# A two-layer graph attention kernel: 128-row transposes and block-diagonal products cut into 64-row tiles, two links of the step loop moved one step later, and the gathers of a group released at two places

## The chip, the cores and the metric

One core of a Trainium2 chip runs the kernel. The time is device microseconds of one execution, as the median of repeated runs. The engines of the core are named as in the profile: PE is TensorE (matrix products and transposes), PEld the loading of its stationary operands, DVE is VectorE, ACT is ScalarE, POOL is GpSimd (it also issues the gathers), and SP is SyncE, which here only issues DMAs.

## The reference

Two graph attention layers over 2048 nodes with the same 0/1 adjacency matrix, for a batch of 8 inputs with 64 features each. The first layer has 4 heads, the second one.

```python
def _gat_layer(h, mask, b):
    scores = jnp.einsum('...nd,...md->...nm', h, h)
    scores = jnp.where(mask, scores, NEG)
    attn = jax.nn.softmax(scores, axis=-1)
    return jnp.einsum('...nm,...md->...nd', attn, h) + b

mask = graph + jnp.eye(N, dtype=graph.dtype) > 0
h = jnp.einsum('bnc,hdc->bhnd', x, Wh)              # 8 x 4 x 2048 x 64
out_h = _gat_layer(h, mask[None, None], bh[None, :, None, :])
z = jax.nn.leaky_relu(cat, negative_slope=0.2)      # cat: the 4 heads side by side
h2 = jnp.einsum('bnk,dk->bnd', z, Wo)               # 256 features back to 64
out2 = _gat_layer(h2, mask[None], bo)
z2 = jax.nn.leaky_relu(out2, negative_slope=0.2)
...                                                 # layer norm, times gamma, plus beta
x = _layernorm(x + out)
```

## The kernel before

The adjacency is sparse but for its first nodes. The kernel treats 56 nodes as hubs, with dense products. The other 1992 nodes are cut into 166 sets of 12. For each set the kernel finds a list of at most 128 nodes that any of the 12 is linked to (the picks: chains of MAX8 and MATCH_REPLACE8 on DVE, L727 to L784), and only those are gathered. A step of the first layer works on one group of two sets, so there are NG = 83 groups; a step of the second layer works on four sets, 42 steps.

In the trace the hub stage lasts from 0 to about 162 us, the first layer's stage (called stage 1 here) from 162 to about 634, a passage between the layers to about 680, and the second layer's stage (stage 2) to about 1017, followed by the end of the layer norms.

A gathered set is a tile `g` of 128 nodes by 4 pairs of batches, with 128 features for each pair (two batches side by side), 64 KB and more. What stage 1 does with group g, in the order of the data:

- **gather** (L790): two indirect DMAs, one for each set, issued by POOL into buffers of a pool of 10, which is 5 groups.
- **turn** (L509): per set four transposes of 128x128, node rows to feature rows, into the PSUM tile with tag T. ACT copies it to `xTg` (L1030).
- **own_rows** (L795, a POOL copy per two groups), **columns** (L802, PE) and **keep_columns** (L808, ACT): the 12 nodes' own rows times the Gram matrix of each head. The stationary operand is block-diagonal: both batches of a pair in one 128x128 product, half of it zeros.
- **scores** (L814, PE, tag S): 32 products on 64x64 tiles, four of them standing abreast in the matrix engine. **weigh** (L824, DVE) subtracts the mask, **lift** (L831, ACT) takes the exponential.
- **values** (L837, PE, tag O): 16 products on 128x64 tiles, two abreast; each pair's first or last column gives the softmax sums. **invert** (L848, DVE) divides.
- **turn_values** (L859, PE): four transposes of 112x128 into a free corner of the same tile of tag O; **keep_values** (L865, ACT, two copies) brings them out.
- **project** (L525, PE, tag C) and **leaky** (L514, ACT), **leak** (DVE): the 4 heads' weights on 64x64 tiles; **second_maps** (L873, PE) and **keep_own** (L882): the second layer's input; **second_rows** (L889, PE, one transpose of 128 rows) and **keep_rows** (L892, DVE): back to node rows, which SP writes to the table that stage 2 gathers from.

The order of the work is written out by hand: a loop `for i in range(-4, NG + 3)` (L1017) interleaves different groups, and each engine runs its instructions in the order in which the loop issues them. In the kernel before, step i issues for PE: scores of group i+1, project of i-1, values of i, second_maps of i-2, second_rows of i-3, columns of i+4, turn of the first set of i+3, turn_values of i, turn of the second set of i+3. The gathers of group i+5 are both issued after values of i, and the buffers they write are those of group i, so they wait for the last product of values(i). PSUM is full: four tags S, C, O and T, each one buffer of two banks. Also in the loop are the list jobs of the later rounds (`some(n)` does n of them; one job is a MAX8 with its MATCH_REPLACE8), parts of the hubs' work in the first eight steps (`slow`), and from step 30 on the loading of x and the adding of beta for the end (`load_own` on SP, `add_beta` on POOL).

In the hub stage `turn_x` (L580) transposes x itself with the same `turn`. In stage 2 `turn2` (L1314) turns two groups a step with the same `turn`, 16 transposes, an ACT copy of 128x1024 behind each eight (L1320); `scores2` (L1126) reads the copies.

Of the kernel before, what the change touches and what calls it, by code (L numbers as in the profile page):

```python
# [44 lines left out]
HUB = 56  # L45
# [314 lines left out]
def fast_kernel(ctx: ExitStack, tc: tile.TileContext, x, adj, Wh, bh, Wo, bo, gamma, beta, out, flag):  # L360
# [148 lines left out]
    def turn(tp, rows):  # L509

        for q in range(Q):
            nc.tensor.transpose(tp[:, q * P:(q + 1) * P], rows[:, q, 1:1 + P], ident)  # L512
# [12 lines left out]
    def project(ot, cat, n):  # L525

        for hp in range(HP):
            for s in range(2):
                for j in range(2):
                    h = 2 * hp + j  # L530
                    nc.tensor.matmul(cat[half(j), s, hp * n:(hp + 1) * n], whT[half(s), h * D:(h + 1) * D],  # L531
                                     ot[half(s), h, :], start=True, stop=True)
# [47 lines left out]
    def turn_x(i):  # L580
        tp = two(f"px{i}")
        turn(tp[:, 0, :], xrow[i])
        nc.scalar.copy(xT[:, :, i * P:(i + 1) * P], tp[:, 0, :].rearrange("c (q n) -> c q n", q=Q))
# [143 lines left out]
    def pick(r):  # L727
# [7 lines left out]
        def top(src, dst, last):  # L735
            def job():
                nc.vector.max(out=dst, in_=src)
                if not last:
                    nc.vector.match_replace(out=src, in_to_replace=dst, in_values=src, imm_value=-1.0)
            return job  # L740

        for j in range(ns):
            for i in range(KEEP // 8):
                k = j * KEEP + i * 8
                todo.append(top(kv[:, j, :], cand[:, k:k + 8], i == KEEP // 8 - 1))
# [7 lines left out]
        for i in range(P // 8):  # L753
            todo.append(top(cand, best[:, i * 8:(i + 1) * 8], i == P // 8 - 1))
# [35 lines left out]
    def gather(table, s, layer, new):  # L790
        t = rows[layer, s] = new(f"g{layer}_{s}")
        nc.gpsimd.indirect_dma_start(out=t.rearrange("n q c -> n (q c)"), out_offset=None, in_=table,  # L792
                                     in_offset=bass.IndirectOffsetOnAxis(ap=index[:, s:s + 1], axis=0))

    def own_rows(m):  # L795

        w = min(4, NS - 4 * m)
        t = held["x", m] = work.tile([P, 2 * GM], F32, tag="xo", name=f"xo{m}", bufs=2)
        src = xT[:, :, HUB:].rearrange("c q (k s) -> c s q k", s=NS)[:, 4 * m:4 * m + w]
        nc.gpsimd.tensor_copy(t[:, :w * 48].rearrange("c (s q k) -> c s q k", s=w, q=Q), src)  # L800

    def columns(g, cat):  # L802

        n = min(4, NS - 4 * (g // 2)) * 48
        for k in range(2):
            nc.tensor.matmul(cat[:, k, 2 * GM:2 * GM + n], gram[:, g % 2 * 2 + k, :], held["x", g // 2][:, :n], start=True, stop=True)  # L806

    def keep_columns(g, cat):  # L808
        n = min(4, NS - 4 * (g // 2)) * 48
# [624 lines left out]
```

## Time and profile before

| what | value |
|---|---|
| median of 14 runs | 1046.41 us (1036.43 to 1052.23) |
| the profiled execution, own time | 1054.11 us |
| its span on the core | 1052.2 us |
| its mean granted PE clock | 0.916 |
| stage 1, 349 to 560 us: PE busy | 207.09 of 211.00 us |
| stage 1, 349 to 560 us: DVE, ACT, POOL busy | 130.84, 135.76, 120.79 us |
| stage 2, 700 to 1000 us: PE busy | 229.55 of 300.00 us |
| stage 2, 700 to 1000 us: DVE, ACT, POOL busy | 163.36, 146.71, 132.04 us |

The profile page lists the busy time of each engine, the chain of work that ended last, and groups of instructions: one row for each line and operation, with the count behind "x", then after a bar the busy time in us and the mean of one in ns, and after a second bar the idle time of that engine just before them and what ended most of it. The timeline lists an engine's blocks in order of time: start in us, duration in us, engine, line, operation, moving and stationary operand, tile of the matrix engine (rows*columns), the instruction's shape, count. Matrix instructions are pipelined, so blocks overlap by the depth of the pipe, and the time of a block is best read from its start to the next block's start. An fp32 product counts as two instructions, a transpose as one.

### The profile page before, as it was taken

Reading aid. Unit: us, or ns where it says so; the run is one execution under the profiler, and the core shown is the slowest. Engines: PE = TensorE matmul, PEld = TensorE weight load, DVE = VectorE, ACT = ScalarE, POOL = GpSimd, SP = SyncE. Lnnn points to the kernel's source line nnn. Section 1 sums busy time; section 2 is a strip of 40 time slices with the busy share of each in tenths; the row PEclk is TensorE's granted clock in tenths of the full one; section 3 lists DMA queues with packets and bytes.
Section 4 is the critical chain, followed back from the end, with each engine's and each line's share of the span. In section 5 each row is a group of like instructions: output and inputs, shape, how many; then the busy total and the mean of one; then the engine's idle time right before and its main releaser. Section 6 shows DMA issues by size and latency. Waiting matters only on the chain.

```text
span 1052.2 us, 42066 instructions
## 1 busy us (share of the span) xinstructions
PE 840.7 (80%) x18437; PEld 709.6 (67%) x18437; DVE 612.8 (58%) x1369; ACT 518.0 (49%) x961; POOL 464.1 (44%) x612
## 2 busy tenths in 40 slices
PE   2977778798999999999999983677787787877740
PEld 2645557687899888888898963466566666666630
DVE  3348844688877777655555553024454555556695
ACT  2322235465666666666666651345444544445541
POOL 5543214564444555555565505344444344444400
PEclk9988889999999999999999995689889899899985
DMA  8775412553344555555555406464555555555521
GB/s 177 226 208 164 123 48 77 150 143 103 98 114 115 146 149 145 153 156 156 153 150 156 126 24 176 131 163 133 153 155 159 152 160 158 143 166 157 162 59 32
DMA packets 81794, 145.22 MB, mean 138 GB/s; under 512 B 30146, under 2 KB 46466, under 8 KB 81602
## 3 DMA queue, kind: packets, MB, share of 16 engines
q0 software_dynamic: 26720, 88.55, 31.4%
q1 hardware_dynamic: 37842, 49.65, 16.3%
q10 hardware_dynamic: 17040, 4.25, 2.2%
q8 instruction: 147, 2.41, 0.9%
q14 instruction: 45, 0.37, 0.1%
HBM read 123.91 MB, written 18.48 MB: 135 GB/s over the span
## 4 chain that ended last, share of the span: by engine, by line
PE 66%; DVE 11%; issue 6%; ACT 6%; DMA 4%; another core or an unknown queue 3%; POOL 1%; SPq 0%; DVEq 0%; ACTq 0%; POOLq 0%
PE t L512 14%; PE s L821 10%; PE o L846 8%; PE cat L806 5%; PE s L1133 5%; PE cat L531 3%; PE o L863 3%; PE o L1165 3%; PE cat L880 3%; ACT xTg L1320 2%; PE sh L1277 2%; PE e L1144 2%; PE cat L890 2%; DVE e L594 1%
## 5 line engine op out<-in xcount | busy, mean ns | idle before, releaser
L792 POOL DMA_INDIRECT g<-table,index x332 | 330.4, 995 | 408.5 <-PE o L846 169.2
L512 PE MATMUL t<-ident,g 128*128 128x128 f32 x1328 | 199.7, 282 | 23.8 <-DMA g<-table,index 12.5
L512 PEld LDWEIGHTS t<-ident,g 128*128 128x128 f32 x1328 | 159.2, 145 | 42.6 <-issue 34.7
L1320 ACT COPY xTg<-t 128x1024 f32<-128x1024 f32 x83 | 80.7, 1016 | 132.3 <-PE t L512 85.4
L826 DVE TENSOR_TENSOR e<-s,mask 128x768 f32<-128x768 f32 x83 | 79.5, 957 | 105.7 <-PE s L821 105.3
L821 PE MATMUL s<-y,xTg 64*64 64x48 f32 x5312 | 115.1, 222 | 4.6 <-issue 3.4
L821 PEld LDWEIGHTS s<-y,xTg 64*64 64x64 f32 x5312 | 98.9, 134 | 24.4 <-issue 15.5
L1152 DVE TENSOR_TENSOR es<-e,linked 128x384 f32<-128x384 f32 (+1 forms) x42 | 23.1, 551 | 144.8 <-PE t L512 93.7
L518 ACT ACTIVATE z<-cat,bhp 128x192 f32<-128x192 f32 x166 | 60.9, 418 | 85.7 <-PE cat L531 85.7
L846 PE MATMUL o<-g,e 128*64 128x65 f32 x2656 | 96.5, 226 | 0.0
L1133 PE MATMUL s<-xTg,bd 128*32 128x128 f32 x1328 | 66.3, 318 | 32.6 <-issue 20.1
L846 PEld LDWEIGHTS o<-g,e 128*64 128x64 f32 x2656 | 84.9, 139 | 9.9 <-issue 0.2
L1030 ACT COPY xTg<-t 128x1024 f32<-128x1024 f32 x83 | 84.1, 1013 | 2.4 <-PE t L512 2.4
L833 ACT ACTIVATE e<-e,shifts 128x768 f32<-128x768 f32 x83 | 79.3, 955 | 2.1 <-DVE e L826 2.0
L1133 PEld LDWEIGHTS s<-xTg,bd 128*32 128x32 f32 x1328 | 43.8, 126 | 50.0 <-issue 40.4
L597 ACT ACTIVATE e<-e,shifts 128x896 f32<-128x896 f32 x32 | 33.4, 1044 | 83.2 <-DVE e L594 68.2
L812 ACT COPY y<-cat 128x384 f32<-128x384 f32 (+1 forms) x80 | 40.7, 508 | 65.9 <-DVE rowt L894 41.5
L680 POOL TENSOR_SCALAR a<-raw 120x1024 bf16<-120x1024 int32 (+1 forms) x34 | 37.9, 1119 | 67.0 <-DMA raw<-in_adj_dram 36.5
L806 PE MATMUL cat<-xo,gram 128*128 128x192 f32 (+1 forms) x320 | 65.0, 326 | 0.0
L1165 PE MATMUL o<-g,es 128*32 128x65 f32 x2656 | 57.7, 244 | 8.1 <-DVE y_s L1188 5.1
L1165 PEld LDWEIGHTS o<-g,es 128*32 128x32 f32 x2656 | 53.0, 126 | 10.5 <-issue 6.2
L853 DVE RECIPROCAL rall<-o 64x8 f32<-64x8 f32 x166 | 34.0, 205 | 44.1 <-PE o L846 42.7
(177 smaller groups left out, 1462.8 us busy)
## 6 DMA issues: line engine op xcount, KB each, us to landing
raw<-in_adj_dram SPq DMA_DIRECT2D x32, 480.0 KB
table<-xb SPq DMA_DIRECT2D x22, 256.0 KB
xr_s<-table SPq DMA_DIRECT2D x21, 256.0 KB
g<-table,index POOLq DMA_INDIRECT x332
table<-x SPq DMA_DIRECT2D x16, 260.0 KB
x<-in_x_dram ACTq DMA_DIRECT2D x32, 128.0 KB
table<-rowt SPq DMA_DIRECT2D x166, 24.4 KB
xb<-in_x_dram SPq DMA_DIRECT2D x164, 24.0 KB
```

Of the source, the lines that this page charges most:

```text
L512: nc.tensor.transpose(tp[:, q * P:(q + 1) * P], rows[:, q, 1:1 + P], ident)
L518: nc.scalar.activation(z[:, hp], cat[:, :, hp * n:(hp + 1) * n], AF.Identity, bias=bhp[:, hp:hp + 1], scale=1.0)
L792: nc.gpsimd.indirect_dma_start(out=t.rearrange("n q c -> n (q c)"), out_offset=None, in_=table, in_offset=bass.IndirectOffsetOnAxis(ap=ind ...
L806: nc.tensor.matmul(cat[:, k, 2 * GM:2 * GM + n], gram[:, g % 2 * 2 + k, :], held["x", g // 2][:, :n], start=True, stop=True)
L821: nc.tensor.matmul(sp[half(r), p, (q * 2 + j) * M:(q * 2 + j + 1) * M], xt[half(p), j, q, half(r)], y[half(p), (j * Q + q) * M:(j * Q + q ...
L826: nc.vector.tensor_tensor(e[:, :16 * M].rearrange("p (a q n) -> p a q n", a=2, q=Q), sp[:, :, :8 * M].rearrange("p a (q n) -> p a q n", q= ...
L833: nc.scalar.activation(e[:, :16 * M], e[:, :16 * M], AF.Exp, bias=shifts[:, 0:1], scale=1.0)
L846: nc.tensor.matmul(op[half(p), j, o0:o0 + K1], e[:, c0:c0 + 64], rw[j][:, q, sums(p)], start=True, stop=True)
L1030: nc.scalar.copy(t, held.pop(("tp", i + 2)))
L1133: nc.tensor.matmul(sp[q * 32:(q + 1) * 32, k, :], bd[u % 3][:, k, q, :], xt[:, s % 2, q, :], start=True, stop=True, tile_position=(0, q * 32))
L1165: nc.tensor.matmul(op[t * 32:(t + 1) * 32, f, k * W2 + p:k * W2 + p + K1], e[:, 2 * q + p, k, :], rw[:, q, sums(p)], start=(a == 0 and k = ...
L1320: nc.scalar.copy(t, tp)
```

## The change

- `turn` makes two transposes of 64 node rows out of each of 128: stationary 64x128, moving a 64x64 identity. The two halves write to two banks of the tile. This holds for stage 1, for the hub stage and for stage 2; the readers take a view (`turned_rows`) in which the halves lie apart.
- `columns` becomes eight products on 64x64 tiles with 96 columns each in place of two block-diagonal products of 128x128 with 192. It writes to the tile of tag O, not C, and stands ahead of values. `own_rows` makes three POOL copies in place of one: half of the rows are also needed with the two batches swapped.
- `turn_values` becomes eight transposes of 48x128 in place of four of 112x128, done one step later (group i-1 in step i) and written to the tile of tag C; `keep_values` is one ACT copy in place of two. Project, leaky and leak (group i-2), second_maps (i-3, into the tile of tag S) and second_rows (i-4, two transposes of 64 rows) follow a step later. The loop runs to NG + 4, one step more.
- The first gather of group i+4 is issued at the start of step i and waits for turn_values of the step before; the second is issued after values(i) and waits for project of step i. Both waits are added by hand.
- A list job is one MAX8 or one MATCH_REPLACE8, not a pair. Six jobs run in each step with i < 0 (none before), three in a step up to 15, then two. `load_own` and `add_beta` start at step 10 and run in four steps of six, not at step 30 in each step in turn.
- PE's order in step i is now: scores i+1, project i-2, columns i+4, values i, second_maps i-3, turn_values i-1, second_rows i-4, turn of both sets of i+3.

On all engines together PE gets 2311 more matrix instructions (664 for the turns of stage 1, 664 for those of stage 2, 64 for `turn_x`, 504 for columns, 332 for turn_values, 83 for second_rows), ACT 83 fewer, POOL 84 more; DVE and SP keep their number.

The diff, cut to what is spoken of:

```diff
-    def turn(tp, rows):
+    def turn(tp, rows, j=0):
         for q in range(Q):
-            nc.tensor.transpose(tp[:, q * P:(q + 1) * P], rows[:, q, 1:1 + P], ident)
+            c0 = (j * Q + q) * 64
+            for r in range(2):
+                nc.tensor.transpose(tp[:, r, c0:c0 + 64], rows[half(r), q, 1:1 + P], ident[half(r), half(r)])
...
-    def gather(table, s, layer, new):
+    def gather(table, s, layer, new, behind=None):
...
+        if behind is not None:
+            tc.add_manual_dep(g.ins, behind.ins.name, mybir.DependencyInfo(mybir.DependencyClass.Sync, mybir.DependencyReason.DATA),
+                              reason="the gather's turn")
...
-        nc.gpsimd.tensor_copy(t[:, :w * 48].rearrange("c (s q k) -> c s q k", s=w, q=Q), src)
+        nc.gpsimd.tensor_copy(v[:, 0], src[:, 4 * m:4 * m + 2])
+        b0 = min(4 * m + 2, NS - 2)
+        for r in range(2):
+            nc.gpsimd.tensor_copy(v[half(r), 1], src[half(1 - r), b0:b0 + 2])
...
-            nc.tensor.matmul(cat[:, k, 2 * GM:2 * GM + n], gram[:, g % 2 * 2 + k, :], held["x", g // 2][:, :n], start=True, stop=True)
+            for r in range(2):
+                for p in range(2):
+                    nc.tensor.matmul(op[half(p), r, Q * OW + k * GM:Q * OW + (k + 1) * GM], gram[half(r), g % 2 * 2 + k, half(r)],
+                                     t[half(r), (p ^ r) * GM:((p ^ r) + 1) * GM], start=True, stop=True)
...
-    def turn_values(g, op):
+    def turn_values(g, pt):
-        osb = held.pop(("o", g))
+        osb = held.pop(("o", g)).rearrange("a j q c -> a (j q c)")
         for w in range(4):
-            nc.tensor.transpose(turned(op)[:, w, :], osb[:112, w].rearrange("a s c -> a (s c)"), ident[:112, :112])
+            for p in range(2):
+                mine = slice(p * 64, p * 64 + M)
+                at = nc.tensor.transpose(pt[:, p, w * M:(w + 1) * M], osb[mine, w * P:(w + 1) * P], ident[mine, mine])
+        return at
...
     def second_rows(g, pr):
-        nc.tensor.transpose(pr, held.pop(("own", g)), ident)
+        t = held.pop(("own", g))
+        for r in range(2):
+            nc.tensor.transpose(pr[:, r, :], t[half(r)], ident[half(r), half(r)])
...
-    LOOK = 5
+    LOOK = 4
...
-    for i in range(-4, NG + 3):
+    for i in range(-4, NG + 4):
+        coming = i + LOOK if i > 0 else i + LOOK + 1 if -2 <= i < 0 else NG
+        if coming < NG:
+            gather(table1, 2 * coming, 1, rows_tile, turned_at)
...
-            project(held.pop(("ot", i - 1)), cat, GM)
+            projected_at = project(held.pop(("ot", i - 2)), cat, GM)
...
+            columns(i + 4, op)
         if 0 <= i < NG:
-            op = one(f"o{i}", "O")
             values(i, op)
-            invert(i, op)
-        if 0 <= i + LOOK < NG and i > -3:
-            for j in range(2):
-                gather(table1, 2 * (i + LOOK) + j, 1, rows_tile)
+        if coming < NG:
+            gather(table1, 2 * coming + 1, 1, rows_tile, projected_at)
...
-        if 0 <= (i - 30) // 2 <= NV:
-            (add_beta if i % 2 else load_own)((i - 30) // 2)
+        if i >= 10 and (i - 10) // 6 * 2 + (i - 10) % 6 // 2 <= NV and (i - 10) % 6 < 4:
+            (add_beta if i % 2 else load_own)((i - 10) // 6 * 2 + (i - 10) % 6 // 2)
+        quota = 6 if i < 0 else 3 if i < 16 else 2
...
+            turned_at = turn_values(i - 1, cat[:, :, 2 * GM:4 * GM])
...
-            turn(tp[:, 0, :], rows[1, 2 * (i + 3)])
-        if 0 <= i < NG:
-            turn_values(i, op)
-            keep_values(i, op)
-        if 0 <= i + 3 < NG:
-            turn(tp[:, 1, :], rows[1, 2 * (i + 3) + 1])
+            for j in range(2):
+                turn(tp, rows[1, 2 * (i + 3) + j], j)
```

## The prediction, made before the changed kernel had run

> **What bounds the kernel now.** I read the table of stretches first, because the busy shares of the whole span mix stages with different limits. Its columns are: stretch, PE busy and its count, PEld, DVE, ACT and POOL in the same way, PE's granted clock, DMA share, GB/s.
>
> ```profile
> 264.00:349.00 85.00, 84.36 (x2201) 76.62 (x2199) 66.19 (x181) 54.65 (x113) 40.12 (x54) 1.00 0.43 110
> 349.00:560.00 211.00, 207.09 (x5334) 185.94 (x5332) 130.84 (x330) 135.76 (x273) 120.79 (x156) 1.00 0.55 153
> 700.00:1000.00 300.00, 229.55 (x4393) 187.85 (x4392) 163.36 (x293) 146.71 (x258) 132.04 (x134) 0.90 0.57 155
> ```
>
> In stage 1 PE is busy for 84.36 of 85 and 207.09 of 211 us at full clock, and no other engine is above 78%. In stage 2 PE is busy for 77%, so there it waits as well. Next comes the chain that ended last, cut to 264 to 349 us: scores L821 23.9%, values L846 19.1%, turns L512 16.7%, columns L806 12.3%, turned values L863 7.7%, and 0.1% issue. It is PE from end to end. Between 700 and 1000 us the turns L512 are 23.0% of the chain (69 us) and the ACT copies behind them, L1320, 8.1%.
>
> Third, PE's timeline of one step of stage 1 (start, duration, and so on to the count):
>
> ```profile
> 312.50 1.37 PE L821 MATMUL s<-y,xTg 64*64 64x48 f32 x63
> ...
> 313.69 0.56 PE L531 MATMUL cat<-otb,whT 64*64 64x96 f32 x15
> 314.19 1.15 PE L846 MATMUL o<-g,e 128*64 128x65 f32 x32
> 315.17 0.50 PE L880 MATMUL cat<-z,woT 128*64 128x96 f32 x8
> 315.60 0.31 PE L890 MATMUL cat<-ident,own 128*96 128x128 f32 x1
> 315.75 0.82 PE L806 MATMUL cat<-xo,gram 128*128 128x192 f32 x4
> 316.40 0.60 PE L512 MATMUL t<-ident,g 128*128 128x128 f32 x4
> 316.84 0.55 PE L863 MATMUL o<-ident,osb 112*128 112x112 f32 x4
> 317.23 0.60 PE L512 MATMUL t<-ident,g 128*128 128x128 f32 x4
> 317.76 0.33 PE L821 MATMUL s<-y,xTg 64*64 64x48 f32 x8
> ```
>
> From each start to the next: scores 1.19, project 0.50, values 0.98, maps 0.43, rows 0.15, columns 0.65, turn 0.44, turned values 0.39, turn 0.53 us. The sum is 5.26 us, and no block waits. So a step lasts as long as PE's own work, and what PE is spared in stage 1 comes off the end until another engine is late.
>
> **The change part by part.** *Rates, from single starts in the same step.* A transpose with 128 moving columns follows the one before it after 109 ns, one with 112 after 95 to 100. Columns (192 moving, one tile) take 163 ns an instruction. All are 0.85 ns a moving column. On 64x64 tiles four instructions stand abreast: project (96 moving) spends 82 ns on four, thus 0.85 ns a column for four tiles together. Scores spend about 58 ns on four with 48 moving columns, and values 58 ns on two with 65. A change of tiling costs about 0.1 us (turn to scores 0.20 for 0.11).
>
> *Columns.* Before, 4 instructions took 0.65 us. After, 16 instructions of 96 columns on 64x64 tiles are project's own shape and stand right behind project with no change of tiling: 4 x 82 ns = 0.33. Project loses the change behind it (0.50 to about 0.36), and columns pay it ahead of values (0.42). Both together go from 1.15 to 0.78: **-0.37 us** a step.
>
> *Turns.* Eight transposes of 109 ns and a change of tiling are 0.97 us. After, 16 halves in two row tiles. The trace has no row tile that is 128 columns wide, so its price is bounded. If halves overlap, as scores' tiles do, a pair lasts for its 64 moving columns, 55 ns: 0.44 + 0.1 = 0.55. If the load of 128 columns paces the pair, L863 is the nearest row: its instructions load 128 columns and follow each other after 95 ns, so the load lasts at most 95 ns, 8 x 95 + 100 = 0.86. If halves don't overlap, 16 x 109 = 1.74 + 0.1 = 1.84. I take 0.55, as L821 shows tiles in both row halves loading and running at once: **-0.42**, with ends -0.42 and +0.87.
>
> *Turned values and rows.* Eight transposes of 48 columns in four pairs: at 58 ns (scores' pace for 48 columns) 0.25 for 0.39, **-0.14**; the ends are 0 (pairs at 95) and 8 x 95 = 0.76, +0.37. Rows are one pair for 0.15: **-0.09**, ends -0.09 and +0.07.
>
> A rule speaks against these two terms. The Trainium skill, page "TensorE: Matmul & The Clock Gate", section "LDWEIGHTS (loading the stationary operand)", says that loading goes by the columns, columns / 1.2 ns, and that 32 rows take as long as 128. By it a half costs 107 ns of loading like the whole, pairs gain nothing if the load paces them, and the sum would end near 1020. The row of L863 (95 ns with 128 columns loaded) lies under that figure, so at least for transposes it doesn't hold in full.
>
> The trace has a row for that side too: early on, at half the pace, L575's products (128 loaded, 112 moving) follow each other every 213 ns, no quicker than transposes with 128 moving at that point, which is a pace by loaded columns. It is a product, L863 a transpose, so I side with L863.
>
> *The sum of a step:* 5.26 - 0.37 - 0.42 - 0.14 - 0.09 = **4.24 us**, -1.02.
>
> *The others in 4.24 us.* ACT: copy 1.01, leaky 2 x 0.42, lift 0.96, columns 0.51, turned values 0.54 = 3.8, less some 0.1 for the copy that goes. DVE: 0.96 + 0.42 + 0.69 + 0.55 + 0.25 + 0.28 = 3.15, and two list jobs (0.41 and 0.50) make 4.06, which just fits; three, up to step 15, make 4.5. POOL: two gathers of 1.0 with 0.3 around each, L886 0.28, own_rows 0.36 + 2 x 0.28 in every second step, 3.3 in all; `add_beta` adds 1.28 in two steps of six, 3.8 on average. SP only issues: two table writes 1.24 and four loads of 0.37 at times, under 3. The hidden work thus has 0.2 to 0.5 us to spare, and where that is gone each 0.1 us costs 8 us over 83 steps.
>
> *The added waits.* The first gather's releaser, turn_values, lies in the step before and has run when POOL arrives. The second waits for project, some 1.6 us into the step; behind it stand own_rows, L886 and `add_beta`. A group must have landed when it is turned, about 1.8 steps (7.6 us) after the first gather and 1.3 (5.5) after the second; gathers land 2.3 to 3.4 us after they start. I cost the waits at 0; with that cover gone, up to 0.5 us a step. DMA goes from 153 to some 190 GB/s, and the hub stage moved 202 in its first 60 us.
>
> *Later steps of the chain.* PE meets turned values, project, maps and rows a step later, so no late ACT or DVE result holds it; nothing is gained, since nothing stalls there now. One more drain step: +2 us.
>
> *Over the stage.* Steps 16 to 82: 67 x 1.02 = 68, of which I keep 64, as some are longer already (5.3 to 5.7 with `load_own` and `add_beta` in them). Steps 0 to 15 carry hub work and three list jobs (DVE 4.5, PE 5.9 in the first nine): I keep about half of 16 x 1.02, 9. Together -73.
>
> *Stage 2.* Each step turns 16 blocks: 16 x 109 = 1.74 us, in the trace 2.2 to 4.2 with stalls that end by issue. Halves save 16 x 54 = 0.87 less the change of tiling, 0.76 x 42 = 32 us if all is on the path. The ACT copies of 1.01 behind the turns don't shrink, and the issue stalls may go by instruction, of which there are now more; I take two thirds, **-21** (ends +49, as below, and -32). In the hub stage `turn_x` is hidden by hub work: 0.
>
> **Sum:** 1054.1 (the profiled execution's own time; span 1052.2) - 73 - 21 + 2 = 962. That execution lies 7.7 above the median of the runs, so 962 - 7.7 = **954** for the median.
>
> **The rivals.** (1) *The load paces the pairs.* For: L575, and L512's and L863's moving columns nearly as many as the loaded. Against: L863. Columns keep -0.37; at 95 ns a pair the turns keep -0.11, else 0. Some 75 full steps: 1054 - 75 x 0.37 to 0.48 + 2, stage 2 0 to -6: 1014 to 1028, so 1006 to 1020 after 7.7. (2) *Another engine or PE's instruction supply becomes the bound.* For: DVE at 4.06 and POOL above 4.24 in some steps; PE issues some 338 instructions and loads a step for 274, in 4.24 us in place of 5.26, and the stalls by issue in stage 2 show that supply can be late. Against: scores alone run 128 in 1.19 us without a hole. At 4.75 us a step: 83 x 0.5 = 41, stage 2 10 to 0: about 1000. (3) *The halves don't overlap,* the slower side: each pays its own 109 or 95 ns. Step: -0.37 + 0.87 + 0.37 + 0.07 = +0.94, x 83 = +78; stage 2 +1.74 x 42 x 2/3 = +49; 1181, so 1173. In stage 1 it decides from about 145 ns a pair (13 pairs x (145 - 115) make up for 0.37). Against it: L821's four tiles share 58 ns.
>
> **How the numbers follow.** Forecast 0.56 (its own range 925 to 985), rival 1 0.15, rival 2 0.20, rival 3 0.09. The low end has all of 83 x 1.02 and 32 on the path: 1054 - 85 - 32 + 2 - 8 = 931, with 11 of spread: 920. The high end takes in rivals 1 and 2 with some spread, 1030. Only rival 3 and little else is outside. A difference of 0.3% is about what a measurement of this kernel can tell from none. Faster than that 0.87 (nearly all of the first three), within it 0.03 (rivals 1 and 2 gone further), slower 0.10.
>
> **What would show it.** In the profile after: in a step of stage 1 turns from start to next start near 0.55, turned values 0.25, project with columns 0.78, steps of 4.2 to 4.3 us, PE still busy above 95%. Right for rival 1: pairs every 95 to 107 ns; for rival 2: PE busy below 92% and DVE, POOL or issue named ahead of PE's blocks; for rival 3: single halves 95 to 109 ns apart. The forecast falls if a step is above 4.5 us, or if turns in stage 2 still take 2 us.

## The result and the profile after

The changed kernel takes 1138.65 us (median of 10 runs, 1128.55 to 1144.11) against 1046.76 for the kernel before: 8.75% longer, ratio 1.0875 with a 95% interval of 1.0846 to 1.0903. The forecast was 954. Its profiled execution takes 1132.33 us, 78 more than that of before. (The latter lies 7.7 us above its kernel's median, so the difference of the medians is 92.)

The page of the changed kernel (engines; then the chain that ended last, by engine and by line):

```profile
PE 829.2 (73%) x21252; PEld 681.3 (60%) x21252; DVE 616.9 (55%) x1369; ACT 566.2 (50%) x878; POOL 482.0 (43%) x696
...
PE 48%; issue 13%; DVE 13%; ACT 8%; DMA 6%; another core or an unknown queue 6%; POOL 3%; SPq 1%; POOLq 0%; DVEq 0%; ACTq 0%
```

PE's busy time fell by only 11.5 us (at a mean granted clock of 0.861 for 0.916, so part of it ran more slowly), its share of the chain fell from 66% to 48%, and "issue", time in which the profile shows nothing that was waited for, rose from 6% to 13%. The table of stretches of the changed kernel:

```profile
349.00:560.00 211.00, 178.96 (x5690) 153.79 (x5687) 123.04 (x319) 142.97 (x212) 112.00 (x171) 0.96 0.48 129
700.00:1000.00 300.00, 207.56 (x4220) 169.96 (x4224) 127.17 (x225) 124.67 (x215) 124.99 (x129) 0.80 0.55 150
```

In the first of these stretches PE was busy for 207 of 211 us before; now it is for 179, and no other engine has come near 211 in its place. Yet the blocks themselves are as short as forecast. PE's timeline of the changed kernel, from a stretch without a stop:

```profile
344.23 0.45 PE L878 MATMUL cat<-ident,osb 48*128 48x48 f32 x8
344.52 0.22 PE L905 MATMUL cat<-ident,own 64*96 64x64 f32 x2
344.58 0.66 PE L514 MATMUL t<-ident,g 64*128 64x64 f32 x16
345.16 1.46 PE L838 MATMUL s<-y,xTg 64*64 64x48 f32 x63
```

From start to start: turned values 0.29 us (before 0.39), rows 0.06, the sixteen halves of both turns 0.58 (before 0.97). What came in is elsewhere in the same trace, PE and POOL together:

```profile
442.62 1.15 PE L862 MATMUL o<-g,e 128*64 128x65 f32 x32
442.72 0.96 POOL L798 DMA_INDIRECT g<-table,index  x1 [0.16 <-issue]
443.60 0.33 PE L893 MATMUL s<-z,woT 128*64 128x96 f32 x2
443.99 0.95 POOL L798 DMA_INDIRECT g<-table,index  x1 [0.30 <-DMA table<-rowt]
444.25 0.42 PE L893 MATMUL s<-z,woT 128*64 128x96 f32 x4 [0.32 <-issue]
445.02 0.28 PE L893 MATMUL s<-z,woT 128*64 128x96 f32 x1 [0.35 <-issue]
445.73 0.29 PE L893 MATMUL s<-z,woT 128*64 128x96 f32 x1 [0.43 <-issue]
```

The eight instructions of second_maps take 2.36 us in place of 0.43. They wait for no semaphore. Two start, then none for 0.6 us; four, then none for 0.6; one, then none for 0.7; one. The stops begin about 1 us after the first gather's start and 0.4 and 1.0 after the second's. I call a stretch of over 0.4 us between two starts on PE (loads included), ahead of an instruction that waits for no semaphore, a **hole**, and counted holes in each trace (their sums shift by a few us with how a wait is told).

POOL has a new wait as well. From the waits of the changed kernel between 349 and 560 us (total us, times, longest):

```profile
POOL xo L812 <- DMA g<-table,index: 43.4, 17, 3.2
```

L812 are the two half copies of `own_rows`, on POOL. In the trace the first of them waits for the semaphores of four gathers, the last of which was issued just ahead of it; the copy of all 128 partitions (L809) has no such wait, nor had the old one. So POOL stands until the gather that it has just issued has landed, in every second step; in most of stage 1 steps of about 4.9 and 6.9 us take turns. ACT's two copies with a new access pattern, in the same window, are longer than before (0.51 us, and 0.54 for the two together that one copy has replaced):

```profile
L827 ACT COPY y<-o 128x384 f32<-128x384 f32 x36 | 31.4, 873 | 36.7 <-PE o L862 15.6 <-PE cat L905 9.0 <-remote 7.9
L884 ACT COPY otb<-cat 128x384 f32<-128x384 f32 x36 | 31.0, 860 | 2.9 <-PE t L514 2.3 <-PE cat L905 0.5
```

Where the 78 us are, by the starts of values in each step and of the transposes of L1166 (L1144 before) in stage 2: steps 0 to 20 of stage 1 +27.9, steps 20 to 80 +31.1 (5.89 for 5.37 us a step), the rest of stage 1 and the passage +3.1, stage 2 +16.8, start and end -0.6. Between two later profiles on one chip (e0, below) the difference is 93 us: +25, +34, +3, +25 and +5 in the same parts. Holes in steps 20 to 80 sum to 63 us (before 4), in stage 2 to 72 (before 35). In stage 2 the granted clock is lower too: 0.84 for 0.91, in e0 0.84 for 0.94.

### The profile page after: what moved, and what is told of

Its sections match the earlier page's. It is cut to its first block, busy times and chain, and to the rows that moved or that the text cites. A ratio compares the mean times of both kernels' runs of the same rounds, so it can differ in the third digit from the quotient of the medians.

```text
span 1130.5 us, 47481 instructions
## 1 busy us (share of the span) xinstructions
PE 829.2 (73%) x21252; PEld 681.3 (60%) x21252; DVE 616.9 (55%) x1369; ACT 566.2 (50%) x878; POOL 482.0 (43%) x696
## 3 DMA queue, kind: packets, MB, share of 16 engines
q8 instruction: 168, 2.75, 1.0%
## 4 chain that ended last, share of the span: by engine, by line
PE 48%; issue 13%; DVE 13%; ACT 8%; DMA 6%; another core or an unknown queue 6%; POOL 3%; SPq 1%; POOLq 0%; DVEq 0%; ACTq 0%
PE o L862 9%; PE t L514 7%; PE s L838 7%; PE s L1155 4%; PE cat L537 4%; PE o L1187 3%; DMA g<-table,index 3%; ACT xTg L1342 2%; PE o L820 2%; PE sh L1299 2%; PE s L893 2%; DMA raw<-in_adj_dram 2%; PE cat L878 2%; ACT y L827 2%
## 5 line engine op out<-in xcount | busy, mean ns | idle before, releaser
L798 POOL DMA_INDIRECT g<-table,index x332 | 323.0, 973 | 331.6 <-PE o L1187 153.0
L514 PE MATMUL t<-ident,g 64*128 64x64 f32 x2656 | 139.2, 237 | 69.9 <-issue 42.9
L514 PEld LDWEIGHTS t<-ident,g 64*128 64x128 f32 x2656 | 111.8, 146 | 92.5 <-issue 78.1
L862 PE MATMUL o<-g,e 128*64 128x65 f32 x2656 | 111.1, 236 | 10.1 <-issue 10.1
L862 PEld LDWEIGHTS o<-g,e 128*64 128x64 f32 x2656 | 95.7, 148 | 24.3 <-issue 15.3
L827 ACT COPY y<-o 128x384 f32<-128x384 f32 x80 | 69.5, 869 | 68.1 <-PE o L862 33.0
L898 DVE COPY own<-s 128x96 f32<-128x96 f32 x83 | 21.3, 257 | 110.5 <-PE s L893 65.2
L812 POOL COPY xo<-xT 64x96 f32<-64x96 f32 x84 | 29.7, 353 | 110.4 <-DMA g<-table,index 103.2
L884 ACT COPY otb<-cat 128x384 f32<-128x384 f32 x83 | 70.9, 854 | 8.8 <-PE cat L905 4.7
L1187 PE MATMUL o<-g,es 128*32 128x65 f32 x2656 | 67.4, 262 | 7.0 <-DVE y_s L1210 3.6
```

What stands on the lines that cost most here:

```text
L514: nc.tensor.transpose(tp[:, r, c0:c0 + 64], rows[half(r), q, 1:1 + P], ident[half(r), half(r)])
L798: g = nc.gpsimd.indirect_dma_start(out=t.rearrange("n q c -> n (q c)"), out_offset=None, in_=table, in_offset=bass.IndirectOffsetOnAxis(ap ...
L827: nc.scalar.copy(held["y", g // 2].rearrange("p (b n) h -> p b h n", b=2)[:, :, h0:h0 + 2, :], op[:, :, Q * OW:Q * OW + 2 * GM].rearrange( ...
L862: nc.tensor.matmul(op[half(p), j, o0:o0 + K1], e[:, c0:c0 + 64], rw[j][:, q, sums(p)], start=True, stop=True)
L884: nc.scalar.copy(ot.rearrange("c h (p m) -> c p m h", p=2), pt.rearrange("c p (m h) -> c p m h", h=H))
L1187: nc.tensor.matmul(op[t * 32:(t + 1) * 32, f, k * W2 + p:k * W2 + p + K1], e[:, 2 * q + p, k, :], rw[:, q, sums(p)], start=(a == 0 and k = ...
```

## The experiments

Three theories. **Supply**: PE runs out of instructions behind a gather's start; slow instructions used to bridge that, and the change made them short. **Half copies**: POOL's wait for landings delays the gathers. **ACT**: its copies hold the step.

Chips differed by more than the change, which the first runs showed. On most, the kernel before takes 1040 to 1050 us (kind A, that of the first profiles); on two it takes 879 (kind B). So a ratio is to the kernel before on the same chip, and step times are compared within a kind. In the table, times in us: medians (e0 before and e14 before are single runs), the ratio with its interval, the first 20 steps of stage 1, the mean of steps 20 to 80, stage 2 (first to last of the transposes named above), and the sums of holes in steps 20 to 80 and in stage 2.

| run | kind | median | ratio | first 20 | step | stage 2 | holes, stage 1 | holes, stage 2 |
|---|---|---|---|---|---|---|---|---|
| before, first profile | A | 1046.8 | 1 | 127.3 | 5.37 | 337.6 | 4.4 | 34.8 |
| changed, first profile | A | 1138.7 | 1.088 | 155.2 | 5.89 | 354.4 | 63.2 | 72.0 |
| e0 before | A | 1040.5 | 1 | 126.9 | 5.37 | 329.0 | 2.5 | 36.6 |
| e0 after | A | 1135.9 | 1.088 (1.079 to 1.097) | 152.0 | 5.93 | 353.9 | 59.8 | 70.3 |
| e2 | A | 1109.9 | 1.062 (1.054 to 1.070) | 151.7 | 6.01 | 332.4 | 46.7 | 37.8 |
| e6 | A | 1107.4 | 1.067 (1.063 to 1.071) | 150.9 | 5.67 | 346.5 | 58.8 | 74.6 |
| e7 | A | 1101.7 | 1.060 (1.057 to 1.062) | 151.0 | 5.65 | 345.3 | 34.1 | 74.6 |
| e8 | A | 1063.6 | 1.023 (1.021 to 1.025) | 128.1 | 5.42 | 347.6 | 6.0 | 74.6 |
| e9 | A | 1081.4 | 1.040 (1.038 to 1.042) | 135.8 | 5.89 | 334.0 | 22.2 | 26.0 |
| e14 before | A | 1050.0 | 1 | 126.4 | 5.40 | 335.6 | 5.0 | 38.1 |
| e15 | A | 1062.1 | 1.016 (1.007 to 1.025) | 128.6 | 5.22 | 356.3 | 39.2 | 68.1 |
| e16 | A | 1112.6 | 1.069 (1.062 to 1.075) | 148.6 | 6.10 | 334.4 | 69.1 | 23.3 |
| e1 (= e6) | B | 915.6 | 1.041 (1.036 to 1.045) | 139.8 | 5.13 | 224.2 | 37.0 | 16.3 |
| e3 (= e8) | B | 894.8 | 1.018 (1.010 to 1.025) | 122.5 | 5.14 | 225.9 | 3.2 | 13.3 |
| e4 (= e7) | B | 901.4 | 1.025 (1.020 to 1.031) | 139.3 | 4.81 | 223.2 | 4.3 | 11.0 |
| e5 | B | 915.7 | 1.043 (1.035 to 1.052) | 130.8 | 5.25 | 225.0 | 48.9 | 13.7 |
| e11 (= e5) | B | 925.4 | 1.049 (1.045 to 1.053) | 130.2 | 5.37 | 228.3 | 51.3 | 14.9 |
| e10 (= e15) | B | 913.3 | 1.036 (1.030 to 1.042) | 131.6 | 5.25 | 222.5 | 47.5 | 11.2 |
| e12 (= e16) | B | 892.9 | 1.014 (1.010 to 1.017) | 132.7 | 4.92 | 217.7 | 9.1 | 1.0 |
| e13 | B | 900.4 | 1.022 (1.017 to 1.026) | 129.2 | 5.17 | 216.2 | 0 | 0 |

**Half copies on DVE (e1, e6).**

```diff
-            nc.gpsimd.tensor_copy(v[half(r), 1], src[half(1 - r), b0:b0 + 2])
+            nc.vector.tensor_copy(v[half(r), 1], src[half(1 - r), b0:b0 + 2])
```

> The changed kernel with the two swapped half copies of own_rows made by DVE in place of POOL. Three theories of the 92 us. Supply: each gather, as it starts its transfers, holds up the supply of PE's instructions for some 0.6 us, and PE, whose instructions are now short, runs out of them; it expects the holes of 0.4 to 0.7 us about 0.7 to 1.1 us behind each gather's start to stay, steps of 5.5 us, time above 1100. Half copies: these copies on POOL wait until all gathers in flight have landed (2.3 to 3.2 us in each second step), so the following gathers are late and come two at once; it expects the alternation of 4.9 and 6.9 us to go, steps of 5.0 or less, the 20 us lost in the early steps back, 1055 or less. ACT: its two copies with a new access pattern (0.87 and 0.85 us in place of 0.51 and 0.54) bring it to 4.4 us a step and hold the step; it expects no change, 1138.

It fell on kind B, where no bound of these could be tested. Again, on kind A:

> The first run's kernel (half copies of own_rows on DVE) again, on this chip, since chips differ: the whole difference of two chips lay in stage 2 and in holes behind the gathers. If this chip gives 1046 or so for the kernel before: half copies expects 1055 or less (the alternation of 4.9 and 6.9 us gone, the early 20 us back), supply 1090 to 1120, since holes stay behind each gather. If it is one that gives 880: 1.04 as before.

The wait and the alternation are gone (most steps last 5.4 to 5.9 us after the early ones) and the ratio falls from 1.088 to 1.067. The half copies cost some 2%; the holes stay (59 us), and so do the early steps (151 us). Half copies as the main cause has fallen.

**Turns alone split, in the kernel before (e3, e8).** The edit of `turn`, with its readers, nothing else.

```diff
-            nc.tensor.transpose(tp[:, q * P:(q + 1) * P], rows[:, q, 1:1 + P], ident)
+            c0 = (j * Q + q) * 64
+            for r in range(2):
+                nc.tensor.transpose(tp[:, r, c0:c0 + 64], rows[half(r), q, 1:1 + P], ident[half(r), half(r)])
```

> The kernel before with the turns alone split into 64-row halves (stage 1, turn_x, stage 2). Half copies and ACT expect the whole gain of the turns, since neither is in it: 1046 less 75 x 0.42 less some 21 in stage 2, about 995. Supply expects part of it to be lost to holes behind the gathers, since the turns no longer cover them: steps of about 5.1, 1015 to 1045. If halves did not overlap, it would be 1150 or more.

> The kernel before with split turns alone, again. On a chip with 1046: stage 1 steps of 5.05 us (as seen on the other chip) where nothing holds PE; supply expects holes in the turns or scores and steps of 5.2 to 5.4, and stage 2 longer by 20 us: ratio 1.01 to 1.02. Half copies: stage 1 shorter by 15 us, stage 2 not longer: 0.98.

Slower by 2% on both kinds, though halves overlap. PE's timeline of e8:

```profile
417.81 0.82 PE L813 MATMUL cat<-xo,gram 128*128 128x192 f32 x4
418.55 0.46 PE L514 MATMUL t<-ident,g 64*128 64x64 f32 x8
418.94 0.60 PE L870 MATMUL o<-ident,osb 112*128 112x112 f32 x4
419.47 0.46 PE L514 MATMUL t<-ident,g 64*128 64x64 f32 x8
419.86 1.33 PE L828 MATMUL s<-y,xTg 64*64 64x48 f32 x58
```

The two turns fall from 0.44 and 0.53 to 0.39 each, but columns now last 0.74 to the next start (before 0.65) and turned values 0.53 (before 0.39), since a tiling begins or ends at each of four borders: 2.05 us in place of 2.01. In the order of the kernel before, the split saves PE nothing. In stage 2 of kind A the holes double from 37 to 75 us, the granted clock falls to 0.86 (0.91 to 0.94 before), and the stage is 10 to 19 us longer.

**Turns whole again, in the changed kernel (e2),** with the two kernels themselves for comparison.

```diff
-            for r in range(2):
-                nc.tensor.transpose(tp[:, r, c0:c0 + 64], rows[half(r), q, 1:1 + P], ident[half(r), half(r)])
+            nc.tensor.transpose(tp[:, j, q * P:(q + 1) * P], rows[:, q, 1:1 + P], ident)
```

> The kernel before, unchanged, for a profile on the chip on which the runs beside it are made (another chip gave 879 us for it where the first gave 1046). Expected on such a faster chip: stage 1 steps of 5.25 us as on the first, and the difference in stage 2. If it is the first chip or one like it, 1046 and the same profile.

> The changed kernel, unchanged, on that chip. If the loss is the half copies of own_rows on POOL, which wait for the gathers in flight, the ratio to the kernel before stays near 1.09 on any chip and the steps alternate. If it is the supply of PE's instructions, it depends on the chip: near 1.04 or 1.05, as with the half copies on DVE, where no holes behind the gathers are seen, and 1.09 where they are.

> The changed kernel with the turns whole again, 128x128 transposes in stage 1, turn_x and stage 2; all else as in the changed kernel. Supply: the slow transposes cover part of the holes; about as long as the changed kernel or up to 30 us shorter. Half copies: PE has slack in the long steps, so the turns cost nothing there; within 15 us of the changed kernel. If PE's own work bounds it, 0.42 x 75 + 20 = 50 us longer.

It is 26 us *faster* than the changed kernel. Of that 21 are in stage 2 (332 for 354), where PE's own waits in 300 us read, for the changed kernel (run e0 after) and for e2:

```profile
PE t L514 <- issue: 26.3, 63, 1.1
```

```profile
PE t L512 <- issue: 6.7, 25, 0.8
```

The granted clock of stage 2 is 0.94 with whole turns and 0.84 with split ones, so halves cost there in two ways, by holes and by a lower clock. Nearly all the holes lie where the clock is full, so the two come on top of each other; how the 21 us divide, and what lowers the clock, isn't shown. Stage 1 is only 4 us longer with whole turns, where 0.42 us a step would make 35: that work of PE's was not on its path.

**Columns whole (e4, e7).** `own_rows`, `columns` and `keep_columns` as before, in the tile of tag O; the core of it:

```diff
-            for r in range(2):
-                for p in range(2):
-                    nc.tensor.matmul(op[half(p), r, Q * OW + k * GM:Q * OW + (k + 1) * GM], gram[half(r), g % 2 * 2 + k, half(r)],
-                                     t[half(r), (p ^ r) * GM:((p ^ r) + 1) * GM], start=True, stop=True)
+            nc.tensor.matmul(op[:, k, Q * OW:Q * OW + n], gram[:, g % 2 * 2 + k, :], held["x", g // 2][:, :n], start=True, stop=True)
```

> The changed kernel with columns as before: two block-diagonal products, one POOL copy of the own rows, the old pattern of the ACT copy; they stay in the tile of tag O ahead of values. Half copies: the waits for landings are gone, steps of 4.24 + 0.4 = 4.65, about 1138 - 20 - 67 x 1.25 = 1035. ACT: 4.1 us a step, no bound, the same 1035. Supply: four slow instructions more for cover, but values, maps and turns are as dense as in the changed kernel, holes stay, steps above 5.2, 1070 or more.

> The changed kernel with columns as before, again, for the same reason. On a chip with 1046 for the kernel before: half copies expects steps of 4.65 to 4.8 and stage 1 shorter than before's by 67 x 0.6 = 40 us; supply expects holes in scores and values behind the gathers, steps of 5.2 or more, ratio 1.03 or more; stage 2, with split turns, 20 us longer than before's by supply (359 to 337 us between the changed kernel and the one with whole turns).

On kind B steps without a hole are 4.62 us, and PE's blocks from start to start add up to just that. So a step does last as long as PE's work where nothing stops PE. (That the forecast's 4.24 + 0.38 gives 4.62 too is luck: project with whole columns takes 1.31 us, 0.52 more than with split ones, and scores 0.97, not 1.19.) On kind A the mean step is 5.65. Holes fall to 34 us, with four slow instructions back behind project.

**A gather moved, in the kernel before (e9).** The second gather of a group is issued at the start of the next step; POOL starts it 0.2 us after scores begin; from step 30 on, when `add_beta` runs, 1.3 us after or at their very start, in turn.

```diff
+        if 0 <= i - 1 + LOOK < NG and i - 1 > -3:
+            gather(table1, 2 * (i - 1 + LOOK) + 1, 1, rows_tile)
```

> The kernel before with one edit: the second gather of a group is issued at the start of the next step, ahead of the first gather of the next group, so that the two starts fall into scores and values in place of maps, rows and columns. Supply: PE's instructions are short there, so holes of 0.4 to 0.7 us appear in values behind the gathers, steps of 5.5 us or more, 15 to 50 us longer. Half copies and ACT: no change, within 4 us.

4% longer for one gather moved. In steps 20 to 29, before `add_beta` begins, one hole opens in scores in each step, 0.7 us behind the moved gather:

```profile
325.31 1.08 PE L821 MATMUL s<-y,xTg 64*64 64x48 f32 x48
325.49 0.97 POOL L792 DMA_INDIRECT g<-table,index  x1 [0.33 <-PE t L512]
326.77 0.44 PE L821 MATMUL s<-y,xTg 64*64 64x48 f32 x13 [0.38 <-issue]
```

These holes measure 0.60 to 0.63 us from start to start, and the ten steps last 5.82 us each where the kernel before takes 5.24. So on kind A a single edit shows it: one gather start among short instructions costs PE 0.6 us. (I had expected the holes in values; they are in scores.) From step 30 on a hole comes in only every second step, 22 us of holes in steps 20 to 80. In the others `add_beta` on POOL now lies beside DVE's leak, which takes 1.73 us in place of 0.55; the ACT copies behind it are late and project waits 0.7 us.

**Gathers behind values again, with half copies on DVE (e5, e11).** With e1's edit, and:

```diff
-    LOOK = 4
+    LOOK = 5
...
-        coming = i + LOOK if i > 0 else i + LOOK + 1 if -2 <= i < 0 else NG
-        if coming < NG:
-            gather(table1, 2 * coming, 1, rows_tile, turned_at)
...
-        if coming < NG:
-            gather(table1, 2 * coming + 1, 1, rows_tile, projected_at)
+        if 0 <= i + LOOK < NG and i > -3:
+            for j in range(2):
+                gather(table1, 2 * (i + LOOK) + j, 1, rows_tile)
```

> The kernel of the first run of this list (half copies on DVE) with both gathers of group i+5 issued behind values(i) and no added waits, as in the kernel before. Supply: the holes move with the gathers, from scores and maps to maps, turned values and turns, and stay as long in sum; within 15 us of the first run. Half copies: within 10 us of the first run. If it was the place or the added waits of the gathers that cost the time, 40 us or more below the first run.

> The changed kernel with the half copies on DVE and both gathers behind values(i) for group i+5, with no added waits, again, on this chip. Place of the gathers: holes behind values hit maps, turned values, turns and scores; steps of 5.5 to 5.7, as with the new places (5.67). The early 20 steps: if it is the gathers' places and the shorter look-ahead, back from 151 to 130 us; if the order of the list jobs and hub jobs, they stay at 150.

Both fell on kind B. Holes stay and the step doesn't gain; the first 20 steps gain 9 us. The place and the added waits of the gathers, by themselves, aren't the main cause there. For kind A these two runs say nothing, as no hole in them follows a gather (see below).

**No gathers in stage 1 (e10, e15).** SP loads 128 consecutive rows at the same places. Other rows are used, the mask is combined by a minimum, and the range check is off, so this computes something else with the same instructions on PE.

```diff
+        if layer == 1:
+            g = nc.sync.dma_start(out=t.rearrange("n q c -> n (q c)"), in_=table[11 * s:11 * s + P, :])
...
-                                .to_broadcast([P, 2, Q, 2 * M]), OP.subtract)
+                                .to_broadcast([P, 2, Q, 2 * M]), OP.min)
...
-        nc.vector.tensor_scalar(fl, pf[0:1, 0, 0:1], P - 0.5, None, OP.is_lt)
+        nc.vector.tensor_scalar(fl, pf[0:1, 0, 0:1], -1.0, None, OP.is_lt)
```

> The changed kernel with the gathers of stage 1 replaced by direct loads of 128 consecutive rows that SP issues, at the same places with the same releases (other rows are used, the mask is combined by a minimum, the range check at the end is switched off). Stage 2 keeps its gathers. Supply by gathers: no holes of 0.4 us or more in stage 1, steps of 4.6 us or less, stage 1 some 75 us shorter than the changed kernel's; stage 2 unchanged at about 350. Supply by DMA traffic of any kind, or by the mere number of PE's instructions: holes stay. Half copies: they no longer wait for gathers, so the alternation goes under either theory. ACT: steps not below 4.5.

> The changed kernel with direct loads by SP in place of the gathers of stage 1, again. On a chip that gives 880 its holes lay 255 or 256 instructions apart, as the pieces of 16 KB in which PE's instructions come, and had nothing to do with gathers. On a chip that gives 1046 the holes lie 0.1 to 1.1 us behind a gather's start, some ten instructions apart: if the gathers open them, the 60 us of holes between steps 20 and 80 fall below 20 us and stage 1 is shorter by 40 us or more; if any DMA traffic or the number of instructions does, 40 us of holes or more stay.

On kind A the early steps fall from 152 to 129 us and the step from 5.93 to 5.22; stage 1, from the first values to the last, is 449 us, 9 shorter than before's 459 on that chip, while the changed kernel's is 58 longer than before's. Stage 2, whose gathers stay, is as slow as the changed kernel's, and that is why the whole is still 1.6% above. The holes that follow gathers are gone. 39 us of another form stay, more than expected: nearly all lie exactly 255 or 256 instructions and loads apart, or a multiple of that. PE's instructions come in such pieces; the page's row for them, of the changed kernel:

```profile
q8 instruction: 168, 2.75, 1.0%
```

2.75 MB in 168 packets are 16 KB each, 64 bytes for each of PE's 42504 instructions and loads. On kind B nearly all holes are of this form, with gathers (e1) or without (e10). In e1 they end 2.2 to 2.8 us after the start of the packet (417.53 to 419.90, for one). This run takes the half copies' waits and 2 us a step of POOL's work away too, so not all of its gain is the holes'; e6 tells how much the half copies are, 0.26 us a step.

**Columns whole, gathers behind values, stage 2 whole (e12, e16); whole turns in stage 1 too (e13).** The edits of e4 and of e5's gathers together (columns are whole, so there are no half copies), and in stage 2 alone the turn as before; e13 has e2's edit of `turn` in its place.

```diff
-                turn(tp, rows[2, 2 * g + j], j)
+                turn_whole(tp, rows[2, 2 * g + j], j)
```

> The changed kernel with columns as before, both gathers behind values(i) for group i+5, and whole turns in stage 2; turns in stage 1 and turned values stay split, and the chain stays a step later. If what is lost comes from dense instructions behind the gathers, the early steps and stage 2, this is near the kernel before: columns give cover behind scores, stage 2 is 330, steps of 5.1 to 5.4: 1030 to 1060. On a chip where the gathers open no holes, faster than before by 3%.

> The same as the last with whole turns in stage 1 and turn_x too: of the change only the split turned values and rows, the later chain, the job order and the earlier beta loads are left. Supply: within 10 us of the last, since the split turns' gain is eaten by holes. PE's own work: 0.42 x 75 = 30 us longer than the last.

> The kernel of run e12 (columns whole, gathers behind values, whole turns in stage 2; stage 1 turns and turned values split, chain a step later) again. On a chip that gives 1040 or more for the kernel before: stage 2 back at 330 us and the early steps at 130, since whole turns and the old gathers are back; steps 20 to 80 between 5.2 and 5.6, since the split turns still stand behind the second gather; ratio 1.00 to 1.02. If places and split turns do not matter and the later chain does, 1.03 or more. On a chip that gives 880: 1.014 as before.

On kind B e12 is the nearest to the kernel before, still 1.4% above; e13 has no hole at all, its steps of 5.15 us are PE's work with whole turns, and it is still 2.2% above. So on kind B holes are not the whole loss. Where the rest lies isn't shown, as the kernel before has no profile there. On kind A I expected 5.2 to 5.6 and got 6.10, nearly the same in each step. Its timeline shows why:

```profile
424.30 0.50 PE L891 MATMUL s<-z,woT 128*64 128x96 f32 x8
424.64 0.98 POOL L803 DMA_INDIRECT g<-table,index  x1 [2.39 <-PE o L860]
424.74 0.45 PE L876 MATMUL cat<-ident,osb 48*128 48x48 f32 x8
425.02 0.23 PE L903 MATMUL cat<-ident,own 64*96 64x64 f32 x2
425.08 0.66 PE L514 MATMUL t<-ident,g 64*128 64x64 f32 x16
425.68 0.61 PE L836 MATMUL s<-y,xTg 64*64 64x48 f32 x17
425.93 0.96 POOL L803 DMA_INDIRECT g<-table,index  x1 [0.30 <-issue]
426.70 0.34 PE L836 MATMUL s<-y,xTg 64*64 64x48 f32 x5 [0.42 <-issue]
427.43 0.84 PE L836 MATMUL s<-y,xTg 64*64 64x48 f32 x41 [0.39 <-issue]
```

Beside it the kernel before (e14), with the same gathers at the same place:

> The kernel before again, for its profile beside the next run. On a chip that gives 880 for it: since the split turns alone had steps of 5.05 us there and were 2% slower, its steps should be 5.0 or less (scores 0.97 in place of 1.19, for PE's instructions are not held behind the gathers), and stage 2 some 225 us. On a chip that gives 1046: as in the first profile.

```profile
415.60 0.97 POOL L792 DMA_INDIRECT g<-table,index  x1 [2.95 <-PE o L846]
415.69 0.31 PE L890 MATMUL cat<-ident,own 128*96 128x128 f32 x1
415.84 0.82 PE L806 MATMUL cat<-xo,gram 128*128 128x192 f32 x4
416.50 0.60 PE L512 MATMUL t<-ident,g 128*128 128x128 f32 x4
416.87 1.05 POOL L792 DMA_INDIRECT g<-table,index  x1 [0.30 <-PE cat L806]
416.93 0.55 PE L863 MATMUL o<-ident,osb 112*128 112x112 f32 x4
417.32 0.60 PE L512 MATMUL t<-ident,g 128*128 128x128 f32 x4
417.85 1.43 PE L821 MATMUL s<-y,xTg 64*64 64x48 f32 x64
```

In both, two gathers start 1.3 us apart after values. Before, rows, columns, turns and turned values stand behind them, 17 instructions of 95 to 163 ns in 2.2 us, and scores begin 1.0 us after the second gather's start. In e16 maps, turned values, rows and turns are over sooner, scores run before and through the second gather, and two holes of 0.6 us open in them in nearly every step. It also shows that gathers at the old place don't help a chain that has become short there.

No version beats the kernel before, on either kind.

## Why the prediction was wrong

*What bounds the kernel:* PE, as read. But scores at 1.19 us already held a stop: without one they take 0.97 (e14 at 412.85, e8 at 414.82). I took that time for PE's work, and read "without a hole" out of it.

*Columns, -0.37:* right. Without a stop project and columns take 0.35 + 0.44 us in the changed kernel, forecast 0.78.

*Turns -0.42, turned values -0.14, rows -0.09:* right. 0.58, 0.29 and 0.06 us, forecast 0.55, 0.25 and 0.06; a pair of halves follows the last after 59 ns. The rule on loading in the Trainium skill ("TensorE: Matmul & The Clock Gate", section "LDWEIGHTS (loading the stationary operand)"), 107 ns for 128 columns, doesn't hold for these transposes. Rivals 1 and 3 are out. But the gain belongs to the new order of the blocks too: e8 shows that in the old order the borders between tilings take it back.

*The sum of a step, 4.24:* near as PE's work; without a stop the blocks of the changed kernel add up to 4.10 us. As the step's length it is what failed: steps 20 to 80 take 5.89 us. That "what PE is spared in stage 1 comes off the end" held only until PE's instructions came too late, and that no engine's busy time tells.

*The others in 4.24 us:* ACT was mis-sized. I kept 0.51 for keep_columns and took 0.1 off 0.54 for keep_values; with the new patterns they are 0.87 and 0.86, and ACT's instructions add up to some 4.5 us a step. They overlap, so ACT is busy for 3.9 us in e15's steps without a hole, which take 4.4. As the main cause the theory falls: e7 has the old pattern of the columns and 5.65.

*Later steps of the chain, "no late ACT or DVE result holds it":* not quite. In a step of e15 without a hole (from 371.55) scores and the wait behind them take 1.27 us, 0.3 more than scores alone: project waits for keep_rows on DVE, and DVE ahead of it for ACT's longer copy of the columns.

*The added waits, "I cost the waits at 0":* failed in a place I had not listed. The half copies of `own_rows`, which I counted as 2 x 0.28 us of POOL's work, carry a wait for every gather in flight. That is some 2% (e6). The added waits themselves were not tested apart on kind A.

*Rival 2, "PE's instruction supply":* this is what happened in steps 20 to 80, and its price (4.75 us a step, about 1000) and its chance (0.20) are the step that failed: in steps 20 to 80 the holes alone make 1.05 us a step, and 5.67 us are left when the half copies' wait is gone (e6). I counted 338 instructions and loads a step; there are 324. I held against it that scores ran 128 of them in 1.19 us without a hole. A high rate in one block says nothing on how long PE can go on when the supply stops; what counts is what PE has to do behind the stop. I also let the halves gain 21 us in stage 2, where stops by issue were already in the profile: they cost 17 to 25 there, by holes and at a lower clock. A page of the Trainium skill that I didn't weigh bears on it: "Runtime: NRT & Kernel Launch", section "Instruction fetch mechanics", says that instructions come in blocks of 256 and that crossing a boundary is mostly hidden. The blocks are as it says; hidden they are not with short instructions (39 us of holes in 60 steps of e15), and the stops behind gathers it doesn't have.

*Steps 0 to 15, -9:* it is +28 by step 20. In these steps holes sum to 15 us (before 4), turns wait 9 us for landings (before 0), and the granted clock is 0.82 (before 0.99). With direct loads they are back at 129 us; in e16, with the gathers at their old place and no half copies, they are not, at 149, though both have a clock of 0.91. How the 28 divide, and why the clock is lower, stays open.

## What to carry to other kernels

A short instruction saves time only if the next ones are there: before splitting matrix work into more and shorter instructions, mark in the timeline where gathers start and see which slow blocks stand behind them, since these may be what bridges a stop. A stop of PE ahead of an instruction without a wait, small in the old profile, is a price to be multiplied, not noise. And of a copy that is split or moved, read the waits that the built program gives it, not only its duration.

## What the runs showed of the hardware

- On chips of kind A, PE starts next to nothing for 0.4 to 0.7 us, once to three times, from 0.1 to 1.1 us after an indirect gather's start, with some ten instructions and loads between. One gather moved into scores makes one such stop a step (e9, steps 20 to 29); without gathers in the stage they are gone (e15). On kind B they don't show. What inside the chip links the two wasn't tried, nor what makes the kinds differ.
- On both kinds PE can stop for 0.4 us or more at places 256 instructions and loads apart; in e1 the stop ends 2.2 to 2.8 us after its 16 KB packet starts. It comes where PE is quick: in e13, with 284 a step in 5.15 us, there is none, in e1, with 324 whose blocks take 4.10 without a stop, 37 us of them lie in 60 steps.
- A border between tilings of the matrix engine costs 0.09 to 0.15 us (e8), so four of them can eat a halved block. The section "Key Properties" of the Trainium skill's page "TensorEngine Tiling (Array Packing)" says that changing the mode drains the engine; it gives no price, these are the prices here.
- In stage 2 on kind A the granted clock was 0.82 to 0.86 with split turns (the changed kernel, e6, e7, e8, e15) and 0.90 to 0.94 with whole ones (the kernel before, e2, e9, e16). Why it falls isn't shown.
- DVE's leak took 1.73 us in place of 0.55 while POOL added two tiles beside it (e9).
